# Two transformer layers on one core: five table loads moved to ScalarE's queue, identity products ahead of the first transposes, and another order of the first steps

## The chip, the core and the metric

The kernel runs on one core of a Trainium2 chip. A core has TensorE (PE, matrix products into PSUM), VectorE (DVE), ScalarE (ACT), GpSimd (POOL) and SyncE (SP, used here to issue transfers), and 16 DMA engines. Each engine runs its own instructions in order and waits for the others through semaphores. The metric is the time of one execution in device microseconds (us), lower is better. All data are 32-bit floats.

## The reference

The input `x` has 4 batches of 512 rows of 512 elements, 2048 rows in all. Two layers follow each other, and each adds an attention and an expert network to its input, both of which read the same normalized rows `xn`:

```python
x = L0_attn_hidden_states
xn = _layernorm(x, axis=-1)
x = x + _L0_attn_ref(xn, ...) + _L0_ffn_ref(xn, ...)
xn = _layernorm(x, axis=-1)
x = x + _L1_attn_ref(xn, ...) + _L1_ffn_ref(xn, ...)
return x
```

The attention of layer 0 has 16 heads of 128 elements. What matters here is its start:

```python
q = (hidden_states @ Wq + bq)                        # 16 heads x 128
q = apply_rope(rmsnorm(q, qn_w), pos)                # rotates the first 64 elements of a head
w_log = (hidden_states @ Wcmp + bcmp).reshape(Bq, C, RATIO)
w_cmp = softmax(w_log, axis=-1)                      # four rows are compressed into one
entries = einsum('bcr,bcrh->bch', w_cmp, hidden_states.reshape(Bq, C, RATIO, HID))
ck = apply_rope(rmsnorm(entries @ Wk + bk, kn_w), block_ends)
cv = entries @ Wv + bv
sc = einsum('bhsd,bcd->bhsc', q, ck) * scale         # then top 8 of the compressed rows, softmax
lk = apply_rope(rmsnorm((hidden_states @ Wlk + blk), kn_w), pos)
lv = (hidden_states @ Wlv + blv)                     # local attention: window of 128 back
out = 0.5 * (sparse + local) @ Wo + bo
```

The expert network of layer 0 picks two of eight experts for each row by `xn @ Wr` and adds their weighted products. Layer 1 has ordinary attention with 16 heads of 32, and an expert network with a projection and a root-mean-square norm. The change doesn't touch them.

## The kernel before, in words

Rows lie in tiles of 128: 16 tiles, four (`TC`) to a batch. A tile of `x` is loaded by SyncE (`load_x`, L139) into `acc`. `layernorm(n, ...)` (L221) has three parts. Statistics are made at once when it is called: BN stats on VectorE (L228), aggregate (L232), an added epsilon (L233), the power -1/2 on GpSimd (L234) and for a tile with `scaled` a product on GpSimd (L236). `rows()` makes the normalized tile `xn`, on ScalarE (L243) or VectorE (L245), and issues its store to `xnd` in memory (L248): by ScalarE for tiles 4 to 7, by SyncE for the others. `turn()` transposes it on TensorE against an identity matrix (L253, four 128x128 transposes) and copies the result into `xnT` on ScalarE (L254).

Attention of layer 0 goes through 32 steps: eight groups of two heads, times four batches. The products of one step (q, local k and local v of two heads: 768 columns from 512 rows and 512 inputs) are not made plainly: they are made as a 2x2 block product with seven instead of eight block products (Strassen's scheme in Winograd's form). `combine_weights` (L110) makes the sums of weight blocks, four VectorE subtractions of 128x768 (L120), and for the fourth of them also the difference of the two biases on GpSimd (L122); `sums_x` (L672) makes the sums of the transposed rows. `product` (L691) is one block product of 128 rows: two instructions with 384 columns. `first`, `second`, `third`, `fourth`, `fifth` and `sevenths` (L731 to L771) use these, `finish` (L701) normalizes and rotates the heads, `turn_queries` (L715) and `turn_keys` (L721) transpose them. `compress` (L599) makes the compressed rows: `wt` transposes (L605), softmax of four (L607 to L614), `wd` (L619), a broadcast product `wB` on TensorE (L622), key and value (L632), `ck` and its transpose `trck` (L642). `scores` makes the score tiles; GpSimd adds the mask of the local window (L813).

A weight block of a group lies in two tiles, `wA` and `wB`, each loaded by `load_block` in two halves of 384 KB. SyncE issues at the start, in this order: four tiles of x, the two halves of wA, the bias bA (192 KB, broadcast over the partitions), `load_tables` (the two norm weights, 64 KB each, and the rotation's cosines and sines, 160 KB each), the two halves of wB, `wr` (router weights), the bias bB, three very small tables, then stores of xn and the other tiles and tables of `rest()` (L1147).

Before the loop over the steps stands the first part, L1165 to L1200, which is the preparation of step 0, written out by hand: `begin()` with the layernorms of tiles 0 to 3, `first(parts())` and so on. Two things set the order that results. An instruction that goes through `tc.keep_in_program_order` keeps its place among the others of its engine that do. All others are placed by the framework's scheduler when the kernel is built. Transfers signal their completion through eight counters that are handed out in turn over the queues of SyncE and ScalarE together; so the issue of a transfer waits until the one eight places earlier has landed.

The matmul of 32-bit data appears in the profile as two MATMUL records for each instruction; a transpose appears as one.

## Time and profile before

| what | value |
|---|---|
| median of 3 runs | 2000.9 us (1999.35 to 2002.6) |
| profiled execution | 2000.65 us |
| its span | 1998.8 us |
| TensorE busy | 1968.6 us (98%) |
| VectorE busy | 1510.7 us (76%) |
| ScalarE busy | 875.3 us (44%) |
| GpSimd busy | 771.0 us (39%) |
| granted TensorE clock | 0.999 |

The span is the time between the first and the last instruction of the profiled execution; the 1.85 us between it and the execution's own time lie around it. Busy time is the union of an engine's instructions, without waits and without the issue of transfers. In the lines of the timeline a row is a group of like instructions that follow each other: its start in us from the span's start, its busy time, the engine, the line, the operation, what it writes and reads, the shape and the number of instructions; a bracket gives the idle time of that engine before it and what ended it. `SPq` and `ACTq` are the issuing queues of SyncE and ScalarE.

### The profile page before, as it was taken

To read this page: it belongs to the slowest core of one execution; us is meant where nothing else is said; L and a number is where in the kernel's file an instruction comes from. 1 tells how busy PE (TensorE), PEld (TensorE's weight loads), DVE (VectorE), ACT (ScalarE), POOL (GpSimd) and SP (SyncE) were. 2 spreads that over 40 slices of the span, in tenths; PEclk is the share of its full clock that TensorE was granted. 3 is DMA by queue.
4 is the path that set the end of the run, shared out by engine and by line. 5 is a ranking of instruction groups with operands and counts; after the bars stand their busy time and mean duration, and the time that the engine had idled before them with its cause. 6 is when DMAs were issued, how large, how long until landed. Compare 5 with 4: busy or idle time off the path is not lost.

```text
span 1998.8 us, 28578 instructions
## 1 busy us (share of the span) xinstructions
PE 1968.6 (98%) x9358; PEld 1241.5 (62%) x9358; DVE 1510.7 (76%) x3694; ACT 875.3 (44%) x2666; POOL 771.0 (39%) x827
## 2 busy tenths in 40 slices
PE   8999999999999999999999999999999999999998
PEld 4666667777777777776667766666434445445443
DVE  7889968777877777787768888889696655666886
ACT  4554444444444444444444545545234332333332
POOL 5423254443433332334442344455204432433551
PEclk9999999999999999999999999999999999999999
DMA  8112133433433334244453222322307775775441
GB/s 259 70 37 59 43 128 136 132 112 98 138 124 120 117 126 139 98 135 159 153 177 106 97 65 75 89 85 74 129 27 263 253 262 185 273 253 173 155 154 68
DMA packets 98910, 267.28 MB, mean 134 GB/s; under 512 B 14400, under 2 KB 27840, under 8 KB 87488
## 3 DMA queue, kind: packets, MB, share of 16 engines
q0 software_dynamic: 27072, 148.91, 22.0%
q1 hardware_dynamic: 70528, 114.34, 17.3%
q10 hardware_dynamic: 1152, 2.10, 0.3%
q8 instruction: 77, 1.26, 0.3%
q14 instruction: 81, 0.66, 0.1%
HBM read 222.05 MB, written 42.73 MB: 132 GB/s over the span
## 4 chain that ended last, share of the span: by engine, by line
PE 87%; DVE 8%; ACT 1%; issue 1%; POOL 1%; DMA 0%; DVEq 0%; SPq 0%; ACTq 0%; POOLq 0%
PE p L691 25%; PE hp_r L533 13%; PE st L805 4%; PE op L888 4%; PE st L1416 3%; PE po L1554 3%; PE cx L1430 3%; PE sp L794 3%; PE qp L1392 3%; PE ox L919 2%; PE o L1499 2%; PE ca L857 2%; PE oz L919 2%; PE trm_r L521 1%; PE trk L721 1%; PE trq L715 1%
## 5 line engine op out<-in xcount | busy, mean ns | idle before, releaser
L533 PE MATMUL hp_r<-we_r,xT_r 128*128 128x512 f32 (+1 forms) x592 | 224.3, 596 | 0.6 <-DVE qk L1405 0.5
L485 POOL DMA_INDIRECT xr_r<-xnd,rows_r x72 | 87.0, 1208 | 347.2 <-PE trm_r L521 308.6
L813 POOL TENSOR_TENSOR lT<-lT,lmask 128x512 f32<-128x512 f32 (+1 forms) x128 | 156.2, 1230 | 109.6 <-ACT lT L809 109.2
L691 PE MATMUL p<-wT,x 128*128 128x384 f32 x512 | 177.0, 488 | 0.5 <-DVE u L749 0.4
L691 PE MATMUL p<-wB,x 128*128 128x384 f32 x512 | 175.3, 487 | 0.0
L691 PE MATMUL p<-wA,xnT 128*128 128x384 f32 x512 | 173.8, 491 | 0.3 <-DVE u L731 0.2
L809 ACT ACTIVATE lT<-st,ss_k 128x256 f32<-128x256 f32 (+1 forms) x256 | 100.8, 442 | 161.6 <-PE st L805 161.5
L1418 ACT ACTIVATE pT<-st 128x1024 f32<-128x1024 f32 x128 | 123.3, 1015 | 59.3 <-PE st L1416 51.1
L533 PEld LDWEIGHTS hp_r<-we_r,xT_r 128*128 128x128 f32 (+1 forms) x592 | 83.2, 170 | 96.1 <-issue 93.6
L691 PEld LDWEIGHTS p<-wB,x 128*128 128x128 f32 x512 | 93.9, 190 | 62.9 <-issue 7.0
L691 PEld LDWEIGHTS p<-wT,x 128*128 128x128 f32 x512 | 93.3, 190 | 63.2 <-issue 7.7
L691 PEld LDWEIGHTS p<-wA,xnT 128*128 128x128 f32 x512 | 95.1, 192 | 60.1 <-issue 1.7
L587 POOL TENSOR_TENSOR ss_q<-ss_q,nhalf 128x4 f32<-128x4 f32 x64 | 68.9, 1077 | 158.1 <-ACT ss_q L584 155.9
L582 ACT ACTIVATE sq_q<-qb 128x128 f32<-128x128 f32 x256 | 79.7, 311 | 87.2 <-DVE qb L756 47.1
L805 PE MATMUL st<-qkT 128*128 128x256 f32 (+1 forms) x512 | 114.8, 353 | 0.1
L550 POOL DMA_INDIRECT row_r<-yd,slot_r x64 | 74.1, 1157 | 74.6 <-DMA yd<-yr_r 21.6
L805 PEld LDWEIGHTS st<-qkT 128*128 128x128 f32 x512 | 92.2, 190 | 10.7 <-issue 0.5
L888 PE MATMUL op<-Wo,cT 128*128 128x512 f32 x208 | 92.9, 593 | 0.4 <-DVE lv L771 0.4
L709 ACT ACTIVATE qb<-qb,ss_q 128x128 f32<-128x128 f32 x256 | 82.1, 392 | 24.5 <-POOL ss_k L586 14.9
L716 ACT COPY qkT<-trq 128x512 f32<-128x512 f32 x64 | 37.6, 587 | 124.2 <-PE trq L715 120.1
L586 POOL TENSOR_SCALAR ss_k<-ss_k 128x2 f32<-128x2 f32 (+1 forms) x96 | 36.0, 375 | 144.7 <-ACT sq_k L582 138.5
L587 POOL TENSOR_TENSOR ss_k<-ss_k,nhalf 128x2 f32<-128x2 f32 (+1 forms) x96 | 88.6, 923 | 8.0
(386 smaller groups left out, 4678.7 us busy)
## 6 DMA issues: line engine op xcount, KB each, us to landing
x<-xsd SPq DMA_DIRECT2D x112, 256.0 KB
yd<-yr_r SPq DMA_DIRECT2D x72, 256.0 KB
wA<-in_wA SPq DMA_DIRECT2D x16, 384.0 KB
wB<-in_wB SPq DMA_DIRECT2D x16, 384.0 KB
xnd<-xn SPq DMA_DIRECT2D x24, 256.0 KB
accd<-acc SPq DMA_DIRECT2D x18, 256.0 KB
acc<-in_x SPq DMA_DIRECT2D x16, 256.0 KB
Wo<-in_Wo SPq DMA_DIRECT2D x8, 512.0 KB
```

Of the source, the lines that this page charges most:

```text
L485: G.indirect_dma_start(out=out, out_offset=None, in_=src, in_offset=at_rows(idx))
L533: PE.matmul(hp[ts(h, m), :], lhsT=xT[:, k, ts(h, m)], rhs=w[:, ts(k, HID)], start=(k == 0), stop=(k == KC - 1))
L582: pin(A.activation(sq, x[:, h, :], AF.Square, accum_out=ss[:, j : j + 1]))
L587: pin(G.tensor_tensor(ss, ss, nhalf[:, 0:n], ALU.pow))
L691: fixed(PE.matmul(p, lhsT=x[:, k, ts(c, P)], rhs=w[:, k, :], start=(k == 0), stop=(k == 1)))
L709: A.activation(x[:, j, :], x[:, j, :], AF.Copy, scale=scale[:, n : n + 1])
L805: PE.matmul(st[:, ds((t % 2) * 256, n)], lhsT=qkT[:, HG + h, ts(t, P)], rhs=qkT[:, h, ds(t * P, n)], start=True, stop=True)
L809: A.activation(lT[:, ds(half * 512 + c * 256, n)], st[:, ds(c * 256, n)], AF.Exp, scale=norm_k[(i, h)][2 * half + c])
L813: G.tensor_tensor(dst, dst, lmask.rearrange("p a w j -> p (a w j)")[:, 0:n], ALU.mult)
L888: PE.matmul(op, lhsT=cT[:, h, ts(t, P)], rhs=wo[:, h, :], start=(h == 0), stop=(h == HG - 1))
L919: PE.matmul(p[:, ts(c, 256)], lhsT=left[:, ts(c, P)], rhs=right, start=new and c == 0, stop=True, skip_group_check=True)
L1418: A.activation(pt[:, ts(pair, 2), :], st, AF.Exp, scale=SCALE1)
```

## The change

Five loads (bA, the two norm weights, cosines and sines) are issued by ScalarE in place of SyncE, after ScalarE's first activation, and in program order. SyncE so issues the halves of wB directly behind those of wA. TensorE gets 9 products of the identity with itself ahead of the turn of tile 0 and 4 between the turns of tile 0 and tile 1; nobody reads their result. In the first part the order of calls changes: the fourth sum of weights (`combine_weights` with 3) is made with the second and third, after `sevenths()` and the turn of the logits; the layernorms of tiles 4 and 5 begin after it; the turn of tile 5 stands behind `fourth()`, and its transposes keep their program order.

```diff
+    def beside(**kw):
+        tc.keep_in_program_order(nc.scalar.dma_start(**kw))
+
     def load_tables():
         for w, src in enumerate(("qn_w", "kn_w")):
-            nc.sync.dma_start(out=nw[:, w, :], in_=a[src].partition_broadcast(P))
-        nc.sync.dma_start(out=cos, in_=a["c_cos"][:, :, 0:R])
-        nc.sync.dma_start(out=sin, in_=a["c_sin"])
+            beside(out=nw[:, w, :], in_=a[src].partition_broadcast(P))
+        beside(out=cos, in_=a["c_cos"][:, :, 0:R])
+        beside(out=sin, in_=a["c_sin"])
...
     b_ = wpool.tile([P, 2, 3 * D], F32, tag="b2", name="b2_0")
-    nc.sync.dma_start(out=b_[:, 0, :], in_=a["bA"][0].partition_broadcast(P))
-    load_tables()
     w_.append(load_block(0, "wB"))
...
-    A.activation(small.tile([P, 8], F32, tag="warm", name="warm", bufs=1), nhalf, AF.Exp)
+    tc.keep_in_program_order(A.activation(small.tile([P, 8], F32, tag="warm", name="warm", bufs=1), nhalf, AF.Exp))
+    beside(out=b_[:, 0, :], in_=a["bA"][0].partition_broadcast(P))
+    load_tables()
...
             for k in range(KC):
-                pin(PE.transpose(tr[:, ts(k, P)], xn[:, ts(k, P)], ident))
+                made_ = pin(PE.transpose(tr[:, ts(k, P)], xn[:, ts(k, P)], ident))
+                if n == TC + 1:
+                    tc.keep_in_program_order(made_)
...
+    warm = psum("sc", "warm")
+
+    def keep_warm(n):
+        for _ in range(n):
+            tc.keep_in_program_order(PE.matmul(warm[:, 0:P], lhsT=ident, rhs=ident, start=True, stop=True))
+
     def begin():
+        keep_warm(9)
         start[0][0]()
         start[1][0]()
         start[0][1]()
+        keep_warm(4)
         start.append(layernorm(2, sp0, psum))
...
     sums_x((0, 1))
-    combine_weights(0, (1, 2))
-    start += [layernorm(n, sp0, psum, True) for n in (4, 5)]
     sevenths()
     turns.pop()()
+    combine_weights(0, (1, 2, 3))
+    start += [layernorm(n, sp0, psum, True) for n in (4, 5)]
...
     second(0)
-    combine_weights(0, (3,))
     second(1)
...
-    for n in (4, 5):
-        start[n][0]()
-        start[n][1]()
+    start[4][0]()
+    start[4][1]()
+    start[5][0]()
     fourth()
+    start[5][1]()
```

In the built program, besides the new products and the five moved loads, the order of instructions differs only among the first 100 to 200 instructions of each engine, which in the profile before lie in the first 90 us; after them each engine has the same instructions in the same order.

## The prediction

> **What bounds the kernel now.** I read the totals of the page, then the chain that ended last, then the table of stretches, and went into the first 65 us, since the edit changes the order of work only there.

> ```profile
> span 1998.8 us, 28578 instructions
> PE 1968.6 (98%) x9358; PEld 1241.5 (62%) x9358; DVE 1510.7 (76%) x3694; ACT 875.3 (44%) x2666; POOL 771.0 (39%) x827
> PE 87%; DVE 8%; ACT 1%; issue 1%; POOL 1%; DMA 0%; DVEq 0%; SPq 0%; ACTq 0%; POOLq 0%
> ...
> 15.00:40.00 25.00, 22.28 (x91) 12.59 (x89) 23.48 (x58) 14.00 (x48) 15.26 (x25) 1.00 0.94 312
> 40.00:62.00 22.00, 18.90 (x100) 12.98 (x99) 20.47 (x73) 12.96 (x46) 14.27 (x15) 1.00 0.32 103
> 62.00:110.00 48.00, 45.87 (x238) 31.96 (x239) 42.19 (x127) 28.67 (x93) 18.52 (x29) 1.00 0.16 61
> ```

> The last three rows are stretches: length, then busy PE, PEld, DVE, ACT, POOL, then PE's clock, the DMA share and GB/s. TensorE is busy 1968.6 of 1998.8 us, so all that can be won is some 30 us of idle time, most of it here and at the very end. From 15 to 40 us the bound is VectorE (23.48 of 25.00). After 62 us TensorE has few gaps (45.87 of 48.00 up to 110; 386.30 of the next 390.00; 500.00 of the next 500.00), so a shift made before 62 us is carried to the end. I count shifts there. Now the rows of the stages:

> ```profile
> 6.81 1.37 SPq L93 DMA_DIRECT2D wB<-in_wB  x2
> ...
> 6.04 1.12 PE L253 MATMUL trx<-ident,xn 128*128 128x128 f32 x4 [6.04 <-DVE xn L245]
> 7.83 1.12 PE L253 MATMUL trx<-ident,xn 128*128 128x128 f32 x4 [0.67 <-ACT xn L243]
> 8.74 2.77 PE L691 MATMUL p<-wA,xnT 128*128 128x384 f32 x4
> 14.35 2.75 PE L691 MATMUL p<-wA,xnT 128*128 128x384 f32 x8
> ...
> 10.63 0.20 DVE L195 TENSOR_SCALAR nws<-nw 128x64 f32<-128x64 f32 x1 [2.05 <-DMA nw<-in_qn_w]
> 12.10 0.20 DVE L195 TENSOR_SCALAR nws<-nw 128x64 f32<-128x64 f32 x1 [1.28 <-DMA nw<-in_kn_w]
> 14.12 0.56 DVE L737 TENSOR_TENSOR qb<-p,u 128x384 f32<-128x384 f32 x1 [1.35 <-PE p L691]
> 15.25 0.99 DVE L120 TENSOR_TENSOR wT<-wB 128x768 f32<-128x768 f32 x1 [0.57 <-DMA wB<-in_wB]
> ...
> 45.88 1.47 POOL L122 TENSOR_TENSOR b<-b 128x384 f32<-128x384 f32 x1 [1.91 <-DMA b<-in_bB]
> 47.31 2.67 POOL L813 TENSOR_TENSOR lT<-lT,lmask 128x512 f32<-128x512 f32 x2
> 56.58 3.12 POOL L813 TENSOR_TENSOR lT<-lT,lmask 128x512 f32<-128x512 f32 x2 [0.21 <-ACT lT L809]
> 59.66 0.56 POOL L234 TENSOR_TENSOR mv<-mv,nhalf 128x1 f32<-128x1 f32 x1
> 60.33 0.99 POOL L236 TENSOR_SCALAR mv<-mv 128x1 f32<-128x1 f32 x1
> 61.35 0.81 ACT L243 ACTIVATE xn<-acc,mv 128x512 f32<-128x512 f32 x1 [1.87 <-POOL mv L236]
> 62.22 0.66 PE L253 MATMUL trx<-ident,xn 128*128 128x128 f32 x4 [2.07 <-ACT xn L243]
> ```

> Each row is start, busy time, engine and group; the bracket gives the idle time before it and what ended it. VectorE waits 2.05, 1.28, 1.35 and 0.57 us before it starts its dense stretch at 15.25, and the last of these waits, the one that sets the start, is for the weight block wB, whose two halves SyncE issues only at 6.81 behind the tables. The second place is at 56.58: GpSimd does both masks before the power (L234) and the scalar (L236) of one layernorm, and TensorE stands 2.07 us for that layernorm's transposes.

> **The change, part by part.**

> (1) Tables to ScalarE, wB behind wA. SyncE loses five issues of 0.47, 0.60, 0.65, 0.69 and 0.61 us, 3.0 us together. ScalarE gets them between its table load (ends 2.0) and xn at 6.96; started at 2.2 they end at 5.2, if the last, which must wait for an earlier x load, isn't late: cover 1.7 us. Beyond it xn, TensorE's turn and the first products are late one for one. wB's first half must now also wait for the bA load, so it is issued perhaps 1 us earlier and not 3. The bytes up to the end of wB stay: x 1.05, wA 0.79, tables 0.66, wB 0.79 MB, 3.28 MB in all; the DMA row in 0.5-us slices has moved that much at about 12.7 us, yet VectorE got wB at 15.25, with engines half busy between 12.5 and 14. So the gain lies between 0 and 2.5 us. [...] I take 0.9, near the issue's own shift; wA may land 1 us later by sharing, which is hidden, as VectorE waits for wB anyway.

> (2) Identity products: 9 instructions, 18 records, ahead of turn 0, which TensorE has idle until 6.04. A 128x128 record costs 0.28 us in the slow turn (1.12/4) and about half of it warm (0.60/4 at 13.92); taken between them, at 0.22, the 18 take 4.0 us, from about 1.6 (the identity is made by then) to 5.7, hidden by that wait; at 0.28 they end at 6.6, 0.6 late, and uncovered they would cost 4.0. The four (8 records) go into the 0.67 us of idle time before turn 1: 1.1 us warm, 1.8 slow, so up to 1.1 us late on xnT of tile 1. They may also quicken the first products: 4 records of 128x384 take 2.77 us at 8.74, where 8 take 2.75 at 14.35, so about 2 us of TensorE time before 13 us is at half rate. [...] The row says that VectorE's last wait is for wB, not for the product, and then the product's 1.35 us of wait only turns into a longer wait for wB: 0. I take 0, with 2 as the end.

> (3) The new order. wT4 and its b2 subtraction come earlier, the statistics of tile 4 and 5 later; VectorE's rows up to the last wd are the same in number, so only its idle 0.31 us (L613) goes: 0.3. Against it, xn_4 and its store by ScalarE are later: the store, issued at 26.89, goes at about 29.3, and ScalarE's xn_6 waits until it has landed, about 4.6 us on (33.9; before, xn_6 ran at 32.42). Queued behind it on ScalarE are the copies of turns and the squares; TensorE waits for trx of tile 6, in place at 34.4 to 34.7 where it stood at 33.95, while p3 behind it still has work in hand. I take 0; uncovered, up to 2.
> Then GpSimd: the subtraction of b2 for the next sums waited 1.91 us for bB at 45.88. SyncE, which no longer waits 3.0 and 1.8 us for the stores of xn, loads bB earlier, and the masks at 47.31 come earlier. TensorE's wait for trck at 51.44, 1.23 us, is fed by VectorE rows that ran long beside those masks; most of it may go, or none: 0 to 1.1. At 56.58 the order becomes mask (1.23 us, the mean of the group on the page), pow 0.56, scalar 0.27, mask. From 56.6 with one mask 1.2, the pow ends near 58.4 and the scalar near 58.8 to 59.9, by how the mask runs; taking the late end, xn ends at 60.8, and the transposes come at 60.8 in place of 62.22, 1.4 earlier. One product of 0.65 us that filled before now lies behind; 0.2 of it shows. I take 1.2, and leave the gain at trck inside it, as time won there is waited for again here; the two add only if GpSimd is earlier too.

> Sum: 0.9 + 0 + 0.3 + 1.2 = **2.4 us**. The profiled execution was 2000.65 us (span 1998.8 and 1.85 around it), 0.25 below the median of the runs, 2000.9. So the span goes to 1996.4 and the median to **1998.5**.

> **The rivals.**
> (A) The front and the masks add up: wB lands 2 us earlier, the product with the faster array keeps pace, and the waits at 51.44 and 62.22 both go. For it: the 3.3 us that VectorE waits for nw and the half-busy engines at 12.5 to 14. Against: wB's issue is tied to bA's landing. 2 + 0.3 + 2.5 = 4.8, with 4 to 7 about it: 1996.1 (1993.9 to 1996.9).
> (B) Hidden: wB lands at 15.2 as before, for the bytes are the same, and the later masks find another wait. -0.5 to +0.5: 2000.9.
> (C) Slower: one mechanism, ScalarE's queue behind the store of xn_4. xn_6 needs that store's buffer; if it lands after about 35 us, VectorE's and TensorE's work behind the turn of tile 6 waits with no cover, and every us beyond is a us at the end: 2 to 6, so 2003 to 2007. For it: that store's issue now also waits for an x load on SyncE's queue, in a stretch with a DMA share of 0.94. Against: TensorE holds 2.75 us of p3 there.

> **How the numbers follow.** Forecast (-0.8 to -4.5) 0.50, A 0.27, B 0.13, C 0.10. A difference of 0.2%, 4.0 us, is about what a measurement of this kernel can tell from none. Faster by more: A, and a quarter of the forecast's case, 0.40; slower by more: most of C, 0.08; the rest, 0.52, within. Range: from 1994.2, which leaves out A's lowest tenth (0.03), to 2002.5, which is above B and below C (0.10). The forecast's own range is 1996.4 to 2000.1.

> **What would show it.** (1) wT of L120 starts at about 14.3 and its wait is still for wB; if it starts at 15 or later, B. (2) the product at 8.74 (4 records) takes under 2 us if the array is warm. (3) xn_6 on ScalarE at 33 to 34 us, and no new wait of TensorE between 33 and 40; a wait of over 2 us there is C. (4) GpSimd's pow between the masks, the transposes of 62.22 at about 58.5 to 59.5 with all shifts in, and a wait under 1 us. The forecast falls if the last product of the first 62 us moves by less than 0.8 or more than 4.5 us, or if anything after 110 us, where the instructions stand in the old order, changes by a us.

## The result, and the profile after

The changed kernel takes 2004.45 us, the median of 12 runs (2002.76 to 2006.65), against 2000.27 us (1999.29 to 2003.01) for the kernel before in the same runs: 1.0018 times as long, with a 95% interval of 1.0010 to 1.0025. It is slower by 4.2 us, where 2.4 us of gain were forecast, and outside the range that was given (1994.2 to 2002.5). The profiled execution took 2004.77 us.

First the page of the changed kernel, its totals and its chain (here and below a selection of lines):

```profile
span 2003.0 us, 28634 instructions
PE 1971.8 (98%) x9384; PEld 1245.4 (62%) x9384; DVE 1514.4 (76%) x3694; ACT 873.9 (44%) x2666; POOL 769.3 (38%) x827
PE 87%; DVE 8%; DMA 2%; ACT 1%; issue 1%; POOL 1%; SPq 0%; ACTq 0%; DVEq 0%; POOLq 0%
```

TensorE is busy 3.2 us longer, and the chain has 2% of DMA in it where it had none. The 26 new records take 4.21 and 1.06 us of busy time, where TensorE had been idle, so they don't explain the span. The table of stretches of the changed kernel (length, busy PE, PEld, DVE, ACT, POOL, then PE's clock, DMA share, GB/s) says where to look:

```profile
15.00:40.00 25.00, 20.56 (x77) 11.50 (x77) 23.31 (x56) 12.97 (x45) 16.76 (x25) 0.93 1.02 341
62.00:110.00 48.00, 44.08 (x233) 31.05 (x234) 41.07 (x137) 27.12 (x86) 17.59 (x30) 1.00 0.17 62
```

From 15 to 40 us TensorE is busy 20.56 us where it was 22.28, and the clock column reads 0.93 where it read 1.00: for a part of this stretch TensorE ran at half its clock (below: a half clock). From 62 to 110 us it is busy 44.08 where it was 45.87.

To see where the time is lost, the TensorE instructions of both profiles were matched by counting from the last one back, and the start in the old profile subtracted from the start in the new one. This shift (positive: later) is -0.2 us at 20 us (of the old profile), +0.3 at 32, +2.7 at 40, +2.4 at 55, +2.0 at 76, +4.4 at 85, and +4.0 at 1990. So the loss has two places, one between 32 and 40 us and one between 76 and 85. From 90 us on the shift stays between +4.0 and +4.9.

The front, in the timeline of the changed kernel:

```profile
1.15 0.40 ACTq L154 DMA_DIRECT2D b<-in_bA  x1
8.47 0.34 ACTq L154 DMA_DIRECT2D cs<-in_c_sin  x1
8.95 0.81 ACT L246 ACTIVATE xn<-acc,mv 128x512 f32<-128x512 f32 x1 [6.72 <-DMA acc<-in_x]
...
2.58 3.70 SPq L93 DMA_DIRECT2D wA<-in_wA  x2
6.32 3.67 SPq L93 DMA_DIRECT2D wB<-in_wB  x2
...
5.91 0.69 DVE L231 BATCH_NORM_STATS2 st<-acc 128x6 f32<-128x512 f32 x1 [1.30 <-DMA acc<-in_x]
14.69 1.34 DVE L120 TENSOR_TENSOR wT<-wB 128x768 f32<-128x768 f32 x1 [0.20 <-DMA wB<-in_wB]
...
10.63 1.53 PE L696 MATMUL p<-wA,xnT 128*128 128x384 f32 x4 [0.16 <-DMA wA<-in_wA]
```

ScalarE's first load goes at 1.15 us, while its table load still runs (0.73 to 2.01), and so among the tiles of x, which SyncE issues at 0.72, 1.17, 1.63 and 2.10: the statistics of tile 1 begin at 5.91 us, where the old kernel began them at 4.44. The issue of the sines waits until 8.47, and xn of tile 1 stands behind it until 8.95 (6.96 before). SyncE's wA and wB take 3.70 and 3.67 us to issue, as their second halves wait too: those of wB go at 6.32 and 9.62 us, where they went at 6.81 and 7.81. In the end wB's sum begins at 14.69, 0.56 us earlier than before.

The first loss, in the timeline of the changed kernel:

```profile
22.37 1.39 POOL L122 TENSOR_TENSOR b<-b 128x384 f32<-128x384 f32 x1
22.94 1.63 DVE L120 TENSOR_TENSOR wT<-wB 128x768 f32<-128x768 f32 x1
24.62 2.85 PE L696 MATMUL p<-wT,x 128*128 128x384 f32 x8 [1.81 <-DVE wT L120]
...
30.98 0.81 ACT L246 ACTIVATE xn<-acc,mv 128x512 f32<-128x512 f32 x1 [1.71 <-DMA acc<-in_x]
33.56 0.31 ACT L587 ACTIVATE sq_q<-qb 128x128 f32<-128x128 f32 x1 [1.47 <-DMA acc<-in_x]
34.68 0.81 ACT L246 ACTIVATE xn<-acc,mv 128x512 f32<-128x512 f32 x1
...
35.55 0.66 PE L256 MATMUL trx<-ident,xn 128*128 128x128 f32 x4 [2.04 <-ACT xn L246]
36.86 1.91 PE L627 MATMUL wB<-wd,ones_sq 128*128 128x512 f32 x2
38.57 2.77 PE L696 MATMUL p<-wB,x 128*128 128x384 f32 x6
```

ScalarE stands twice, 1.71 and 1.47 us, at the issue of a store of xn, for a load of x that has nothing to do with the store but is eight transfers ahead of it. The xn of tile 6 comes at 34.68, and TensorE waits 2.04 us for it. In the kernel before it came at 32.42:

```profile
32.42 0.82 ACT L243 ACTIVATE xn<-acc,mv 128x512 f32<-128x512 f32 x1 [0.92 <-DVE qb L756]
```

Then TensorE's own work is slow: six records of 128x384 take 2.77 us, where six take 2.10 elsewhere. The table of stretches, cut at the changes of the clock:

```profile
33.08:36.50 3.42, 1.38 (x10) 1.01 (x9) 3.39 (x14) 2.67 (x11) 1.29 (x3) 1.00 1.10 369
36.50:39.91 3.41, 3.41 (x7) 1.48 (x6) 2.46 (x5) 3.29 (x11) 2.55 (x3) 0.50 0.92 317
```

A stretch of 3.41 us in which TensorE was busy 1.38 us is followed by one of the same length at clock 0.50.

The second loss, in the timeline of the changed kernel:

```profile
60.12 0.74 POOL L237 TENSOR_TENSOR mv<-mv,nhalf 128x1 f32<-128x1 f32 x1 [1.74 <-DVE mv L236]
63.24 0.66 PE L256 MATMUL trx<-ident,xn 128*128 128x128 f32 x4 [1.70 <-ACT xn L246]
...
76.52 1.78 POOL L592 TENSOR_TENSOR ss_q<-ss_q,nhalf 128x4 f32<-128x4 f32 x1 [11.10 <-ACT ss_q L589]
78.27 0.81 PE L696 MATMUL p<-wB,x 128*128 128x384 f32 x2
81.15 0.66 PE L256 MATMUL trx<-ident,xn 128*128 128x128 f32 x4 [2.07 <-ACT xn L246]
```

and the same place in the timeline of the kernel before:

```profile
74.39 1.03 POOL L587 TENSOR_TENSOR ss_q<-ss_q,nhalf 128x4 f32<-128x4 f32 x1 [10.75 <-ACT ss_q L584]
76.47 2.10 PE L691 MATMUL p<-wB,x 128*128 128x384 f32 x6
78.40 0.60 PE L253 MATMUL trx<-ident,xn 128*128 128x128 f32 x4
```

Before, three products (six records) stood ahead of a turn and covered the time until its xn came; now one stands ahead and the others behind, and TensorE waits 2.07 us. The xn is later too: GpSimd makes the power of the heads' norms (L592, L587 before) ahead of the tile's own power, and it takes 1.78 us where it took 1.03. The clock reads 1.00 in the table from 62 to 110 us.

### The profile page after: what moved, and what is told of

Same layout as the page of the kernel before. It is cut to its first block, busy times and chain, and to the rows that moved or that the text cites. A ratio compares the mean times of both kernels' runs of the same rounds, so it can differ in the third digit from the quotient of the medians.

```text
span 2003.0 us, 28634 instructions
## 1 busy us (share of the span) xinstructions
PE 1971.8 (98%) x9384; PEld 1245.4 (62%) x9384; DVE 1514.4 (76%) x3694; ACT 873.9 (44%) x2666; POOL 769.3 (38%) x827
## 3 DMA queue, kind: packets, MB, share of 16 engines
q10 hardware_dynamic: 2384, 2.75, 0.4%
## 4 chain that ended last, share of the span: by engine, by line
PE 87%; DVE 8%; DMA 2%; ACT 1%; issue 1%; POOL 1%; SPq 0%; ACTq 0%; DVEq 0%; POOLq 0%
PE p L696 25%; PE hp_r L538 13%; PE st L810 4%; PE op L893 4%; PE st L1429 3%; PE po L1567 3%; PE cx L1443 3%; PE qp L1405 3%; PE sp L799 3%; PE ox L924 2%; PE o L1512 2%; PE ca L862 2%; PE oz L924 2%; PE trm_r L526 1%; PE trq L720 1%; PE trk L726 1%
## 5 line engine op out<-in xcount | busy, mean ns | idle before, releaser
L592 POOL TENSOR_TENSOR ss_q<-ss_q,nhalf 128x4 f32<-128x4 f32 x64 | 69.6, 1088 | 156.7 <-ACT ss_q L589 154.5
L587 ACT ACTIVATE sq_q<-qb 128x128 f32<-128x128 f32 x256 | 79.3, 310 | 87.1 <-DVE qb L761 45.1
L592 POOL TENSOR_TENSOR ss_k<-ss_k,nhalf 128x2 f32<-128x2 f32 (+1 forms) x96 | 89.0, 927 | 8.0
```

The source lines that it names most:

```text
L587: pin(A.activation(sq, x[:, h, :], AF.Square, accum_out=ss[:, j : j + 1]))
L592: pin(G.tensor_tensor(ss, ss, nhalf[:, 0:n], ALU.pow))
```

## Experiments

The question was which part costs, by what mechanism, and why single executions of one kernel lie up to 4 us apart. Medians are over 11 runs each. Each ratio is to the kernel before, measured beside it (2000.34 us for the first four, 2000.45 for the next four, 2000.65 for the last three).

| kernel | median us | ratio, 95% interval |
|---|---|---|
| tables alone | 2000.82 | 1.0003 (0.9994 to 1.0012) |
| identity products alone | 2001.10 | 1.0004 (0.9995 to 1.0013) |
| new order of calls alone | 2002.77 | 1.0012 (1.0003 to 1.0021) |
| tables and identity | 2001.32 | 1.0008 (0.9999 to 1.0017) |
| order: sums only | 2000.64 | 1.0000 (0.9991 to 1.0009) |
| order: turn of tile 5 only | 2000.42 | 0.9999 (0.9990 to 1.0008) |
| order, four buffers of xn | 2005.09 | 1.0022 (1.0013 to 1.0031) |
| order, biases later | 2003.42 | 1.0015 (1.0006 to 1.0024) |
| all but the turn of tile 5 | 2002.94 | 1.0009 (1.0000 to 1.0018) |
| all but the sums | 2003.44 | 1.0014 (1.0005 to 1.0023) |
| identity, wB ahead of the sines | 2003.83 | 1.0015 (1.0006 to 1.0024) |

### Each part alone

The first kernel takes the loads of the change, and nothing else of it:

```diff
-            nc.sync.dma_start(out=nw[:, w, :], in_=a[src].partition_broadcast(P))
+            beside(out=nw[:, w, :], in_=a[src].partition_broadcast(P))
...
-    nc.sync.dma_start(out=b_[:, 0, :], in_=a["bA"][0].partition_broadcast(P))
-    load_tables()
     w_.append(load_block(0, "wB"))
...
```

> Only the loads are changed: five tables on ScalarE's queue, wB directly behind wA; order of calls and TensorE's work as before. Theory O (the loss comes from the new order of calls): -0.5 to +1.5 us against the kernel before; the first sum of weights starts at 14.7 to 16 us, and no clock drop after 15 us. Theory T (the loss comes from the tables, which overtake the x tiles and leave ScalarE behind): +2.5 to +4.5 us. Either way tile 1 of x arrives at about 5.9 us where it came before 4.4.

Measured: +0.5 us at the median, within the noise. In the timeline of this kernel tile 1 of x comes late again, and the products, still slow (four records take 2.77 us at 11.29 us and 1.67 at 14.71; 1.46 in the second run), are now what VectorE waits for:

```profile
6.03 0.69 DVE L231 BATCH_NORM_STATS2 st<-acc 128x6 f32<-128x512 f32 x1 [1.60 <-DMA acc<-in_x]
16.42 0.56 DVE L740 TENSOR_TENSOR qb<-p,u 128x384 f32<-128x384 f32 x1 [1.76 <-PE p L694]
```

The first sum of weights starts at 16.89 us, 1.6 later than before and behind this wait, no longer behind wB. So the tables don't shorten the front; in this profile they lengthen it by 2.3 us at 20 us, of which 1.2 are left at 60.

The second takes the identity products alone:

```diff
     def begin():
+        keep_warm(9)
         start[0][0]()
         start[1][0]()
         start[0][1]()
+        keep_warm(4)
```

> Only the 13 identity products are added. Theory O: between -1.5 and +0.3 us: the 4 records of the first product take about 1.5 us where they took 2.77, and VectorE's wait of 1.35 us for them goes, but the wait of 0.57 us for wB grows instead. Theory T: the same. A gain above 1.5 us would say that the slow clock of the first 13 us was on the path after all.

Measured: +0.8 us, within the noise. The four records of the first product take 1.46 us where they took 2.77, as expected, and the wait moves to wB in full, as the row of this kernel's timeline shows (VectorE waited 1.35 us for the product and 0.57 for wB before):

```profile
15.87 0.99 DVE L120 TENSOR_TENSOR wT<-wB 128x768 f32<-128x768 f32 x1 [1.83 <-DMA wB<-in_wB]
```

The third takes the new order of calls alone:

```diff
-    combine_weights(0, (1, 2))
-    start += [layernorm(n, sp0, psum, True) for n in (4, 5)]
     sevenths()
     turns.pop()()
+    combine_weights(0, (1, 2, 3))
+    start += [layernorm(n, sp0, psum, True) for n in (4, 5)]
...
-    combine_weights(0, (3,))
...
+    start[5][0]()
     fourth()
+    start[5][1]()
```

> Only the order of calls: the fourth sum of weights earlier, layernorms 4 and 5 later, the turn of tile 5 behind the fourth stage. Theory O: +3 to +5 us, with TensorE's wait for xn of about 2 us near 34 us, a clock of 0.5 for some 3.4 us behind it, and a second wait for xn near 79 us. Theory T: within 1 us of before, TensorE's waits at 34 and 79 us gone, as the store of tile 4 is issued without a wait on a tile of x.

Measured: +2.4 us, slower with an interval clear of 1. Both waits are there (2.08 us at 35.85, 2.06 at 81.44), and so is the half clock from 36.27 to 39.68. That is below the 3 to 5 us that theory O expected, and most of the loss all the same. The store of tile 4 is issued at once here, yet its landing is waited for, as the timeline of this kernel shows:

```profile
34.98 0.81 ACT L243 ACTIVATE xn<-acc,mv 128x512 f32<-128x512 f32 x1 [2.51 <-DMA xnd<-xn]
35.85 0.76 PE L253 MATMUL trx<-ident,xn 128*128 128x128 f32 x4 [2.08 <-ACT xn L243]
```

So theory T's reading of the wait (an issue held by a load of x) is not needed for it: with the tables on ScalarE the queue is held at the issue, without them xn waits for its buffer; TensorE's wait is as long (2.08 and 2.04 us).

The fourth is the change without its new order of calls, both other parts together.

> The change without its new order of calls: tables on ScalarE and identity products. Theory O: -0.2 to -1.5 us against before (VectorE's first sum of weights starts at 14.7 us, 0.5 earlier, and the rest follows). Theory T: +2.5 to +4.5 us.

Measured: +1.0 us by the medians and +1.6 by the ratio, not clear of the noise, where -0.2 to -1.5 was expected of theory O, so the front's gain isn't there. The shift is +0.3 us at 20 us, 0.0 at 60, and +1.6 from 70 on. This step of 1.6 us has one cause in its profile. The table of stretches of this kernel, cut at the clock's changes:

```profile
58.77:62.18 3.41, 1.34 (x6) 0.46 (x4) 3.41 (x23) 1.33 (x4) 2.39 (x3) 1.00 0.00 0
62.18:65.59 3.41, 3.41 (x10) 2.34 (x11) 0.39 (x2) 2.19 (x5) 0.82 (x2) 0.50 0.20 77
```

and the same wait in the kernel before, cut in stretches of the same length from its own change of clock:

```profile
57.47:60.88 3.41, 2.68 (x9) 1.27 (x7) 3.41 (x23) 1.87 (x7) 3.31 (x4) 1.00 0.00 0
60.88:64.30 3.42, 2.08 (x13) 1.60 (x14) 1.94 (x9) 2.20 (x6) 1.27 (x3) 1.00 0.20 77
```

Both kernels wait 2.07 us before the turn at 62.2. In the one the wait falls into one stretch, TensorE is busy 1.34 of 3.41 us, and the next stretch runs at half clock; in the other the wait is cut by the border of two stretches, which are busy 2.68 and 2.08 us, and nothing follows. The price of the half clock is 1.6 us here, in two executions that are alike around it.

### The halves of the new order

The fifth and sixth kernels take the sums, and the turn of tile 5, each alone.

```diff
-    combine_weights(0, (1, 2))
-    start += [layernorm(n, sp0, psum, True) for n in (4, 5)]
     sevenths()
     turns.pop()()
+    combine_weights(0, (1, 2, 3))
+    start += [layernorm(n, sp0, psum, True) for n in (4, 5)]
...
-    combine_weights(0, (3,))
```

> Of the new order of calls only the sums: the fourth sum of weights with the second and third, layernorms 4 and 5 behind them. In the built order TensorE has three products ahead of the turn at about 78 us, as before. Theory S (two separate losses: the late tiles 4 to 6 near 34 us with the halved clock behind them, and the turn at 78 us that lost its products): only the first loss, +0.5 to +2.5 us against before, and no wait of 2 us near 79 us. Rival B (the loss is one, and the second wait only its echo): the whole loss, +2.4 us or more, with the wait at 79 us.

```diff
+                if n == TC + 1:
+                    tc.keep_in_program_order(made_)
...
-    for n in (4, 5):
-        start[n][0]()
-        start[n][1]()
+    start[4][0]()
+    start[4][1]()
+    start[5][0]()
     fourth()
+    start[5][1]()
```

> Of the new order of calls only the turn of tile 5, moved behind the fourth stage, with its transposes pinned. In the built order TensorE has one product ahead of the turn at about 78 us, as in the changed kernel. Theory S: no wait near 34 us, no clock drop there; a wait of some 2 us near 79 us, so +0.5 to +2.5 us against before. Rival B: within 1 us of before, since without the late tiles there is nothing to echo.

Measured: +0.2 and 0.0 us. Theory S, two losses of which each half carries one, falls: neither half costs. Rival B falls for the fifth kernel, which it gave the whole loss. With the sums alone, tile 5 is turned ahead of the products of the fourth stage, tile 6 is normalized at 33.63 us, and TensorE's waits are 0.24 and 0.91 us there; three products stand ahead of the turn at 79 us, and it isn't waited for. With the turn alone, xn of tile 6 is there at 32.20 and the turns wait nowhere near 34 us. One product stands ahead of the turn at 78 us, as in the changed kernel, and it isn't waited for either: GpSimd's power takes 1.13 us there. In all five profiles with both halves of the new order it takes 1.78 to 1.80 us, and the turn is waited for by 2.06 to 2.08. Why GpSimd's row is longer there stays open. So without the tables and the identity products the loss needs both halves.

The ninth and tenth are the whole change without the one half and without the other (in the tenth the two sums and the layernorms also stand ahead of `sevenths()` again).

Against the changed kernel, the ninth:

```diff
-    start[4][0]()
-    start[4][1]()
-    start[5][0]()
+    for n in (4, 5):
+        start[n][0]()
+        start[n][1]()
     fourth()
-    start[5][1]()
```

> The whole change except that the turn of tile 5 stays ahead of the fourth stage. Theory J (neither half of the new order costs alone; together they leave TensorE three waits of 1.2 to 2.1 us at 34, 63 and 81 us, and each can bring a halved clock for 3.4 us on top, worth 1.7 us): within 1.3 us of before, 3 us below the changed kernel. Rival T (the tables on ScalarE cost, in company with any reordering, because its queue stands at an issue): +2.5 us or more against before.

and the tenth:

```diff
-    combine_weights(0, (1, 2, 3))
+    combine_weights(0, (1, 2))
...
     second(0)
+    combine_weights(0, (3,))
     second(1)
```

> The whole change except that the sums of weights and the layernorms of tiles 4 and 5 keep their old order. Theory J: within 1.3 us of before. Rival T: +2.5 us or more, with ScalarE's store of tile 4 or 5 waiting at its issue for a load of x.

Measured: +2.3 and +2.8 us, more than theory J allowed, and near rival T. For the ninth the profile shows rival T's mechanism:

```profile
31.57 0.81 ACT L246 ACTIVATE xn<-acc,mv 128x512 f32<-128x512 f32 x1 [2.39 <-DMA acc<-in_x]
32.43 0.66 PE L256 MATMUL trx<-ident,xn 128*128 128x128 f32 x4 [2.04 <-ACT xn L246]
```

ScalarE stands 2.39 us at the issue of tile 4's store for a load of x, and TensorE waits 2.04 us for the turn of tile 5, with a half clock behind it from 33.06 to 36.47 (eight records take 4.44 us at 32.92 us and 2.74 at 27.21). For the tenth it does not: no wait of TensorE is over 1 us between 30 and 105 us; its shift is +1.5 us at 20 us (late tiles of x) and +1.4 at 120, and 2 us more come at 1532 us, in that one execution, where TensorE waits for a load of expert weights. Why its median is 2.8 us above stays open. The tests of the parts fit a plain sum as well (by the medians tables and identity +1.0, order +2.4, together 3.4 of 4.2; by the ratios 1.6, 2.4 and 4.0 of 3.6), since each has an interval of about 1.8 us to both sides. So it isn't shown whether the parts only add up or act on each other.

### The two suspected waits

The seventh kernel is the third with four buffers for xn.

```diff
-... tag=tag, name=f"xn_{n}", bufs=bufs)
+... tag=tag, name=f"xn_{n}", bufs=4 if tag == "xn" and pool is sp0 else bufs)
```

> The new order of calls alone (as in the third run), with four buffers for xn in place of two, so that xn of tile 6 doesn't wait until the store of tile 4 has landed; the first 80 us of each engine are otherwise in the same order. Theory C (the store's landing): xn of tile 6 runs at 33.3 us, when GpSimd has made its scalar, where it ran at 34.98; TensorE's wait before the turn of tile 6 falls from 2.08 to about 0.6 us, the clock isn't halved at 36 us, and the time is 1.5 to 3 us below the third run. Rival L (the statistics of tile 6 are late anyway, or the broadcast matrix wd is): within 0.8 us of the third run.

Measured: 2005.09 us, slower than the third run by 2.3 where 1.5 to 3 less was expected. The mechanism did what theory C said, and the time didn't. In the timeline of this kernel

```profile
25.09 4.54 PE L693 MATMUL p<-wT,x 128*128 128x384 f32 x8 [1.74 <-DVE wT L120]
35.07 1.07 PE L253 MATMUL trx<-ident,xn 128*128 128x128 f32 x8
...
34.62 0.81 ACT L243 ACTIVATE xn<-acc,mv 128x512 f32<-128x512 f32 x1 [0.89 <-POOL mv L236]
```

xn of tile 6 no longer waits for a landing but for GpSimd, and the turns of tiles 5 and 6 follow each other without a wait (eight records). But this execution had its half clock earlier, from 25.68 to 29.10, behind the waits of 0.65, 0.61 and 1.74 us: eight records take 4.54 us where they take 2.85. That is 1.7 us, and it seems to delay tile 6's statistics too, so that a part of the first loss is paid here: the shift at 40 us is +1.2 where it was +3.0. A second half clock follows the wait at 80 us (2.07 us; eight records take 3.88 us at 81.43, and 2.75 at 57.60), and one more wait stands at 99 us. One profile can't say how much of the median each makes.

The eighth is the third with GpSimd's difference of the biases at its old place.

```diff
-        if 3 in which:
+        if 3 in which and g:
...
     second(0)
+    tc.keep_in_program_order(G.tensor_tensor(b_[:, 1, :], b_[:, 1, :], b_[:, 0, :], ALU.subtract))
     second(1)
```

> The new order of calls alone, with GpSimd's difference of the biases back behind the first of the second stages; nothing else moves. Theory P (the GpSimd subtraction lengthens a VectorE sum that runs beside it: 1.55 us where its like takes 0.95): that sum takes 0.95 us again and the fourth sum ends 0.6 us earlier; the time falls by 0 to 0.8 us against the third run. Without it: the sum stays at about 1.5 us and the time within 0.3 us of the third run.

Measured: 2003.42 us, 0.65 above the third run and not below it. Theory P is right about the row: the sum that took 1.55 us takes 0.95, TensorE's wait for the fourth sum is 1.14 us (1.74 in the third run), and the wait for tile 6 falls to 1.22, as the timeline of this kernel has it:

```profile
21.79 0.95 DVE L120 TENSOR_TENSOR wB<-wB,wA 128x768 f32<-128x768 f32 x1
23.79 2.85 PE L693 MATMUL p<-wT,x 128*128 128x384 f32 x8 [1.14 <-DVE wT L120]
33.89 0.66 PE L253 MATMUL trx<-ident,xn 128*128 128x128 f32 x4 [1.22 <-ACT xn L243]
```

This execution had no half clock before its end (its mean granted clock is 0.999, eight records take 2.75 us at 79.21), and its shift at 40 us is -0.7 us: up to there the new order without it is no loss. The wait at the turn near 78 us is there all the same (2.08 us, with GpSimd's power at 1.80), and the shift goes from -0.9 at 76 to +1.5 at 85. It took 2001.65 us, the lowest of the eleven; the highest took 2006.41.

### The same kernel twice, and one more version

> The changed kernel again, for a second profile of it. Theory K (the clock is judged in fixed stretches of 3.41 us whose phase against the program is random, so that the same wait of 2 us halves the clock in one execution and not in another): the waits near 34, 63 and 81 us are there again within 0.3 us, but the stretch at half clock stands elsewhere or is missing, and the time differs by about 1.7 us for each one. Rival: the half clock stands at 36.5 to 39.9 us again, as a property of the program.

The changed kernel's second profile took 2006.12 us. The rival falls and theory K holds for the place of the half clock, which isn't at 36.5 us; the wait before tile 6's turn is missing too. The table of stretches of this second execution, and its slow products in the timeline:

```profile
22.17:25.59 3.42, 1.47 (x8) 0.91 (x7) 3.42 (x6) 0.59 (x2) 1.87 (x2) 1.00 1.05 318
25.59:29.00 3.41, 3.41 (x7) 1.77 (x6) 2.68 (x10) 0.39 (x2) 0.47 (x1) 0.50 1.05 398
...
24.91 4.54 PE L696 MATMUL p<-wT,x 128*128 128x384 f32 x8 [1.81 <-DVE wT L120]
```

The same wait of 1.81 us for the fourth sum was followed by a half clock here and by full clock in the first execution (1.00 from 22.85 to 36.50 us), and two more stand at 8.52 and 80.20 us. The shift is +1.0 us at 40, +5.1 at 85. That the place is random, two executions don't show. K expected two things that aren't so. The wait near 34 us isn't there again, as the slow products gave tile 6 time to arrive. And two half clocks more, at 1.7 us each, should have made 3.4 us; the executions differ by 1.35.

How much the half clock makes of the medians can be read from the granted clock that is on record for each execution. Its mean is 0.9978 over the 12 executions of the changed kernel and 0.9992 over 93 of the kernel before. A half clock of 3.41 us takes 0.00085 from such a mean, so the changed kernel has some 1.6 of them more in an execution, at most 2.7 us at 1.7 us each (an estimate; those that hide a wait, or fall where nothing waits for TensorE, cost less). And it loses without them: with 0.00085 for one, an execution that is listed at 1.000 had none before its end. 27 executions of the kernel before are listed so, and took 1998.33 to 2000.51 us, 1999.88 at the median. The one of the changed kernel took 2002.91, one of the ninth kernel 2003.86, two of the tenth 2003.39 and 2003.44. So, as far as one execution tells, about 3 us of the 4.2 come without a half clock. For the spread within one kernel, too, the clock is only a part: over all 227 executions of all kernels with a clock on record it goes with about a quarter of the variance within a kernel, and its three decimals hide some of what it explains.

The last version left the tables to SyncE and issued wB ahead of cosines and sines, with the identity products:

```diff
-        nc.sync.dma_start(out=cos, in_=a["c_cos"][:, :, 0:R])
-        nc.sync.dma_start(out=sin, in_=a["c_sin"])
...
     w_.append(load_block(0, "wB"))
+    nc.sync.dma_start(out=cos, in_=a["c_cos"][:, :, 0:R])
+    nc.sync.dma_start(out=sin, in_=a["c_sin"])
```

> No table moves to ScalarE: the kernel before with the identity products, and with wB issued by SyncE ahead of the cosines and sines (behind bA and the norm weights); all engines in the order of before. If the first stage is bound by wB's landing alone, the first sum of weights starts 1 to 2 us earlier than 15.25 and the time falls by 0.5 to 1.5 us. If it is bound by the bytes and by the tables behind, within 0.5 us of before: the rotation then waits for the sines.

Measured: +3.2 us, which neither case had. wB's sum starts at 14.13 us, 1.1 earlier, and it helps nothing, for what lies next is late. In the timeline of this version:

```profile
14.64 1.03 POOL L200 TENSOR_TENSOR t<-cs,nws 128x256 f32<-128x256 f32 x1 [5.46 <-DMA cs<-in_c_cos]
19.18 0.79 DVE L594 TENSOR_TENSOR r<-qb,t 128x384 f32<-128x384 f32 x1 [1.83 <-POOL t L200]
23.98 1.09 PE L715 MATMUL trq<-ident,qb 128*128 128x128 f32 x4 [3.08 <-DVE lg L983]
```

GpSimd starts its rotation tables when the cosines are there, 1.9 us later than before, VectorE waits for them, TensorE waits 3.08 us for VectorE, and two stretches at half clock (23.06 to 29.89) follow: eight records take 5.27 us at 24.86 where they take 2.85 at 16.30. No version that was run beats the kernel before by more than the noise.

## Why the prediction was wrong, point by point

**The clock was taken for a thing of the first 13 us.** The prediction read the granted clock as full from there on and priced every wait at its own length. In the first profile of the changed kernel the clock was full for 30.72 us up to 36.50, then half for 3.413 us, a ninth of that, and full again. In the stretch ahead of a half clock TensorE (matmul records) was busy 1.38 of 3.42 us there, 1.33 of 3.41 in the third run (from 32.86 us), 1.34 of 3.41 in the fourth (58.77), and 1.47 of 3.42 and 1.34 of 3.41 in the second execution of the changed kernel (22.17 and 76.79). Behind 1.64 of 3.41 us (from 22.85 in the first profile of the changed kernel) and 2.08 of 3.42 (from 60.88 in the kernel before) the clock stayed full, and so it did behind these two:

```profile
21.22:24.64 3.42, 1.76 (x12) 1.36 (x12) 3.39 (x7) 1.37 (x5) 1.20 (x2) 1.00 0.78 233
58.77:62.18 3.41, 1.45 (x5) 0.57 (x3) 3.41 (x24) 1.39 (x4) 2.53 (x4) 1.00 0.00 0
```

Both stretches are of the second kernel, whose clock reads 1.00 from 15 to 110 us. With TensorE busy for 1.45 us the clock stayed full here, and with 1.47 us it fell in another program's execution, so these rows give no busy time that decides; what decides isn't shown. In the fourth run the half clock behind a wait of 2.07 us cost some 1.6 us on top. Between 15 and 105 us the old kernel has one wait of over 1.5 us, of 2.07; the new one has four, of 1.70 to 2.07.

**Part 1, front: 0.9 us forecast, 0.2 us in the profile, nothing in the medians.** The step that failed is the cover of 1.7 us: the loads were placed behind ScalarE's table load at 2.2 us, but the first went at 1.15, and three of the five moved in among tiles 1 to 3 of x, ahead of wA as well as wB. The issue of the sines then waited until 8.47 us, where all five were to be issued by 5.2, with xn of tile 1 behind it at 8.95 where it was at 6.96. No run shows the 0.9 us: the first sum of weights started 1.6 us later with the tables alone (the first run) and 0.56 earlier with the whole change, and neither was faster.

**Part 2, identity products: 0 taken, and right.** Turn 0 and turn 1 were later because of x. The quicker products (1.46 us for four records, 2.77 before) moved their wait to wB, as argued; no run shows a gain near the 2 us that were put as the end of the range. Behind the late tiles of the tables they did help: at 20 us the shift is +2.3 with tables alone and +0.3 with both.

**Part 3, the new order: a gain of 0.3 us forecast, a loss of some 2.4 measured (the third run).** The step "I take 0; uncovered, up to 2" failed. The place and mechanism of rival C, ScalarE's queue behind the store of tile 4, are what the first profile shows, at 34.68 us where 33.9 was put; C had a chance of 0.10, and its 2003 to 2007 us held the result. The third run has the wait too, at 34.98 us, and there it is the store's landing itself. Two terms were missing from C's working: the halved clock, and the VectorE sum that runs 1.6 to 1.7 times as long beside GpSimd's subtraction (1.63 and 1.55 us for 0.95), which makes the fourth sum and all statistics behind it late.

**Part 3, masks: 1.2 forecast, nothing measured.** The power did move ahead of the masks. The step that failed is its time: it was to end near 58.4 us and began at 60.12, for it waited 1.74 us for VectorE's addition (L236), which stood behind the top-8 rows; TensorE waited 1.70 us and then 0.56 again, 2.26 in all where it had waited 2.07, and had one product less to fill with.

**What no step had.** The turn at 81 us: 2.4 us by the shift from 76 to 85 us. Its fillers went from three products to one, and GpSimd's power ahead of it took 0.75 us longer; the sixth run shows that fewer fillers alone cost nothing there. The prediction stopped counting shifts at 62 us because few gaps followed there before, though the order was known to differ up to 90 us.

The statement that nothing changes by a us after 110 us held: the shift is +4.5 at 120, +4.9 at 1535 and +4.0 at 1990.

## What to carry to other kernels

A wait of TensorE cost time in two ways here: the new one of 2.07 us near 81 us came with a shift of 2.4 us at full clock, and the half clock behind one of 2.07 us cost 1.6 us on top (the fourth run). The waits themselves seem the larger part: about 3 us of the 4.2, estimated above from single executions without a half clock. So count the waits of 1.5 us and longer that a new order makes, and what stands ready to fill them, before the microseconds that it saves. The loads that went to another queue moved their bytes ahead of loads issued later on the first one (the statistics of tile 1 began at 5.91 us, 4.44 before), and what followed in program order on the new queue's engine stood behind an issue that had to wait (xn of tile 1 at 8.95 us, 6.96 before). Where the total is nearly all one engine's busy time, an order that was fitted by hand is disturbed at places that the edit doesn't name: compare the built orders to the end of the last difference, and price each turn there.
